# One uneven product for a Householder step, and the work laid around it

## The chip, the core and the metric

The kernel runs on one core of one Trainium2 chip. The core has five engines that run side by side and wait for each other by semaphores: TensorE (PE in the profile; its weight loads are shown apart, as PEld), VectorE (DVE), ScalarE (ACT), GpSimd (POOL) and SyncE (SP), which here issues the DMAs. The metric is the time of one execution on the device, in microseconds (us), as the median of several runs. All data are fp32, and an fp32 matmul is carried out as two passes, so the profile shows every product twice.

## The reference, cut to what matters

A stack of four graph layers works on `x` of 128 x 64 x 256. The stretch that is changed lies in layers 0 and 1:

```python
# layer 0: h = relu(layernorm(x))
agg = jnp.einsum('nm,bmd->bnd', A_hat, h)                 # "mix": 64 x 64 matrix over the nodes
h = relu(batchnorm(agg.reshape(-1, 256) @ W1.T + b1))     # 8192 rows, 256 -> 512
out = batchnorm(h @ W2.T + b2)                            # 512 -> 256
# layer 1: needs the eigenvectors of a 64 x 64 symmetric matrix
_, U = jnp.linalg.eigh(L_norm)
```

`L_norm` depends on the adjacency matrix alone, and layer 0 does not need `U`. Layer 1 needs both the result of layer 0 and `U`.

## The kernel before

**Two streams at once.** `eigenvectors` (line 1593) makes `U` while layer 0 is computed. The eigenvector work is a long chain of small operations on 64 x 64 matrices. First `tridiagonal` brings the matrix to tridiagonal form in 62 Householder steps (`householder`, line 1041, c = 63 down to 2). Then `vectors` (line 1426) finds the eigenvalues and eigenvectors, forms `U`, and `verdict` checks the result. At the end a value is loaded from the verdict, and all engines take a branch on it (line 1618), behind which layer 1 begins. Layer 0 is work with full-size products: for each of 16 blocks of 512 rows, `hidden_block` normalises (4 ScalarE operations), mixes (2 groups of 4 products with `BDH`), multiplies by `W1` (8 products of 512 columns), and takes the results out with 4 VectorE statistics and 4 ScalarE copies. When all 16 are done, and the batch statistics with them, `features0` does 8 products with `W2` for each block. In the profile these products are `ps<-BDH,z` and `ps<-z,w`.

**A Householder step.** The matrix `A` lies on 64 partitions. All 64 partitions of the row tiles hold the same row, so each partition can do the scalars of the step by itself. `x` is the current row of `A`. ScalarE squares and sums it and takes the square root `s0`. VectorE forms `r` = 1/s0, `t` = r·h + s0, `NB` = q·t (q is half the sign), corrects two elements of `x` with `OA` and `NB`, and takes a reciprocal, `KAP`. ScalarE makes `uk` = KAP·x. PE has meanwhile made two products with `A` over c rows: `z`, the row that is next, and `y` = xA, with the column of `A` that equals the row x as weights. VectorE combines them to `uA` = NB·z + y, sums uA·uk to `c2`, and makes `v` = c2·x - uA. Then come two things. PE makes the rank-two update as two products with one row each (K = 1), uk by v and v by uk, summed in PSUM, and VectorE adds that to `A`. And VectorE makes the next row by itself, in two updates of `z` with `uk` and `v`. Each step also stores its row x to `V` by a DMA on SP's queue (line 1064).

**What sets the order.** The order on PE, VectorE and ScalarE is written out ahead, by a planner (`Plan`, line 843). `chain` places the operations of the chain one after the other, each with an assumed busy time of its engine and an assumed time until its result is ready. Before each it fills the engine with pieces of layer 0 (`beside`), as far as they end no more than a slack after the chain's operation could start. The slacks are 0.6 us on T (PE), 0.3 on S (ScalarE) and 0.3 on V (VectorE). `emit` sorts all by the planned start and issues them, and each engine keeps that order (`Ordered`). These times only choose an order. What isn't placed by the end of the 62 steps is issued behind `vectors` (`rest`), where the order is not fixed by hand.

Of the kernel before, what the change touches and what calls it, by code (L numbers as in the profile page):

```python
# [8 lines left out]
F32 = mybir.dt.float32  # L9
# [775 lines left out]
GRID = 64  # L785

# [56 lines left out]
class Plan:  # L843
# [55 lines left out]

    def rest(self):  # L900

        while any(self.queue.values()):
            for e in self.queue:
                self.fill(e, 1e9)
# [8 lines left out]
class Fast:  # L913
# [31 lines left out]
    def sum(self, out, a, s, b, op0, op1=ALU.mult, name="junk"):  # L945

        w = a.shape[-1]
        j = self.t(f"{name}{a.shape[0]}", a.shape[0], 64)
        self.o.stt(j[:, 0:w], a, s, b, op0, op1, acc=out)
# [3 lines left out]
    def constants(self):  # L953
# [6 lines left out]
        self.P = t("P", 64, 1)  # L960
        iota(self.P[:], [[0, 1]], 0, 1)
# [21 lines left out]
        o.ts(self.low[:], self.J[:64, :], self.P[:], ALU.is_lt)  # L983
# [3 lines left out]
        o.copy(pi[:], self.P[:])  # L987
# [15 lines left out]
    def tridiagonal(self, S, made, plan):  # L1003
# [3 lines left out]
        A = self.A = t("A", 64, 64)  # L1007
# [3 lines left out]
        for x in (KAP, NB, V):  # L1011
            nc.vector.memset(x[:], 0.0)
        s0, r, tt, q, c2 = (t("h_" + x, 64, 1) for x in "s0 r t q c2".split())
        ja = t("ja", 64, 64)
        bc = lambda c, n=64: c.to_broadcast([n, 64])
        now = {}
        go = plan.chain

        def keep(name, a, b):
            now[name] = self.mm((a, b))  # L1020

        d = go("T", lambda: keep("p", S, self.JR[:]), [made], 0.3, 0.5)
        d = go("V", lambda: o.copy(m[:], now["p"][:]), [d], 0.15, 0.28)
        d = go("T", lambda: keep("p", self.JR[:], m[:]), [d], 0.3, 0.5)
        rest = go("V", lambda: o.copy(A[:], now["p"][:]), [d], 0.15, 0.28)
        d = go("T", lambda: keep("p", bc(ident[:64, 63:64]), A[:]), [rest], 0.3, 0.5)

        def first():
            x = now["x"] = self.rows.tile([64, 65], F32, name="f_x", bufs=8)
            o.copy(x[:, 0:63], now["p"][:, 0:63])  # L1030

        def square(w):
            x = now["x"]
            self.act(ja[:, 0:w], x[:, 0:w], AF.Square, accum_out=x[:, w:w + 1])

        row = go("V", first, [d], 0.15, 0.28)
        h = go("S", lambda: square(63), [row], 0.34, 0.42)
        for c in range(63, 1, -1):
            row, h, rest = self.householder(c, now, go, row, h, rest, (s0, r, tt, q, c2), square)

    def householder(self, c, now, go, row, h, rest, scalars, square):

        o, nc, t = self.o, self.nc, self.t
        ident = self.k.ident
        A, NB, OA, KAP, V = self.A, t("NB", 64, 64), t("OA", 64, 64, 2), t("KAP", 64, 64), t("V", 64, 64)
        s0, r, tt, q, c2 = scalars
        bc = lambda a, n=64: a.to_broadcast([n, 64])
        x = lambda a, b: now["x"][:, a:b]
        nb = NB[:, c - 1:c]
        e, w = 0.001 * c, c - 1  # L1050

        def zy():
            now["zp"] = self.ps.tile([64, 64], F32, name="fps")
            nc.tensor.matmul(now["zp"][:, 0:c], bc(ident[0:c, c - 1:c], c), A[0:c, 0:c], start=True, stop=True)
            now["yp"] = self.ps.tile([64, 64], F32, name="fps")
            nc.tensor.matmul(now["yp"][:, 0:c], bc(A[0:c, c:c + 1], c), A[0:c, 0:c], start=True, stop=True)

        def row_z():
            now["z"] = self.rows.tile([64, 64], F32, name="f_z")
            self.act(now["z"][:, 0:c], now["zp"][:, 0:c], AF.Copy)  # L1060

        def row_uk():

            nc.sync.dma_start(V[c:c + 1, 0:c], now["x"][0:1, 0:c])
            now["uk"] = self.rows.tile([64, 64], F32, name="f_uk")
            self.act(now["uk"][:, 0:c], x(0, c), AF.Copy, scale=KAP[:, c:c + 1])

        def row_uA():
            now["uA"] = self.rows.tile([64, 64], F32, name="f_uA")
            o.stt(now["uA"][:, 0:c], now["z"][:, 0:c], nb, now["yp"][:, 0:c], ALU.mult, ALU.add)  # L1070

        def row_v():
            now["v"] = self.rows.tile([64, 64], F32, name="f_v")
            o.stt(now["v"][:, 0:c], x(0, c), c2[:], now["uA"][:, 0:c], ALU.mult, ALU.subtract)

        def outer():
            uk, v = now["uk"], now["v"]
            p = now["p"] = self.ps.tile([64, 64], F32, name="fps")
            nc.tensor.matmul(p[0:c, 0:c], uk[0:1, 0:c], v[0:1, 0:c], start=True, stop=False)
            nc.tensor.matmul(p[0:c, 0:c], v[0:1, 0:c], uk[0:1, 0:c], start=False, stop=True)  # L1080

        def row_x():
            now["x"] = self.rows.tile([64, 65], F32, name="f_x", bufs=8)
            o.stt(x(0, w), now["uk"][:, 0:w], now["v"][:, w:c], now["z"][:, 0:w], ALU.mult, ALU.add)


        z = go("T", zy, [rest], 0.34, 0.42)
        sq = go("S", lambda: self.act(s0[:], x(c, c + 1), AF.Sqrt), [h], 0.13, 0.23)
        oa = go("S", lambda: self.act(OA[:, c, 1:2], x(c - 1, c), AF.Copy), [row], 0.12, 0.22)
        zs = go("S", row_z, [z], 0.15, 0.26 + e)  # L1090
        sg = go("V", lambda: o.ts(q[:], x(c - 1, c), **halve(0)), [row])
        d = go("V", lambda: o.recip(r[:], s0[:]), [sq])
        d = go("V", lambda: o.stt(tt[:], r[:], x(c, c + 1), s0[:], ALU.mult, ALU.add), [d, h])
        b = go("V", lambda: o.mul(nb, q[:], tt[:]), [d, sg])
        d = go("V", lambda: o.stt(x(c - 1, c + 1), OA[:, c, :], nb, x(c - 1, c + 1), ALU.mult, ALU.add), [b, oa])
        d = go("V", lambda: o.recip(KAP[:, c:c + 1], x(c, c + 1)), [d])
        uk = go("S", row_uk, [d], 0.16, 0.32 + e)
        d = go("V", row_uA, [zs, b, z], 0.12 + e, 0.25 + e)
        d = go("V", lambda: self.sum(c2[:], now["uA"][:, 0:c], 0.5, now["uk"][:, 0:c], ALU.mult), [uk, d],
               0.2 + e, 0.28 + e)  # L1100
        v = go("V", row_v, [d], 0.15 + e, 0.26 + e)
        p = go("T", outer, [v], 0.25, 0.45)
        if c > 2:
            row = go("V", row_x, [v], 0.15 + e, 0.22 + e)
            row = go("V", lambda: o.stt(x(0, w), now["v"][:, 0:w], now["uk"][:, w:c], x(0, w), ALU.mult, ALU.add),
                     [row], 0.15 + e, 0.25 + e)
            h = go("S", lambda: square(w), [row], 0.28 + e, 0.36 + e)
        rest = go("V", lambda: o.add(A[0:c, 0:c], A[0:c, 0:c], now["p"][0:c, 0:c]), [p], 0.12 + e, 0.22 + e)
        return row, h, rest

    def reflectors(self):
# [8 lines left out]
        self.sum(kc[:], self.KAPs[:], 1.0, ident, ALU.mult)  # L1120
# [22 lines left out]
    def scale(self):  # L1143

        o, nc, t = self.o, self.nc, self.t
        NB, A = t("NB", 64, 64), self.A
        self.KAPs = t("KAP", 64, 64)
        DM, NE = t("DM", 64, 64), t("NE", 64, 64)
        o.mul(DM[:], A[:], self.k.ident[:64, :64])
        pe = self.mm((self.k.ident[:64, 1:2].to_broadcast([64, 64]), A[:]))  # L1150
# [293 lines left out]
P = 128  # L1444
# [21 lines left out]
class Kernel:  # L1466
# [126 lines left out]
    def eigenvectors(self):  # L1593
# [3 lines left out]
        with ExitStack() as ex:  # L1597
            fast = Fast(self.tc, ex, self)
            fast.constants()
            plan = Plan(dict(T=0.6, S=0.3, V=0.3), 5)  # L1600
# [206 lines left out]
    def hidden_block(self, i, r, m, plan, needs, used):  # L1807
# [9 lines left out]
        def mix(dc):  # L1817
# [969 lines left out]
```

## Time and profile before

| what | us |
|---|---|
| median of 3 runs (lowest, highest) | 2329.3 (2326.33, 2331.57) |
| span of the profiled execution | 2325.1 |
| first row x copied, first Householder step begins | 11.5 |
| hidden features of layer 0 done (last product) | about 208 |
| last update of A by a step | 272.2 |
| verdict (f_k_badi) | 364.66 |
| first work behind the branch | 370.1 |
| PE busy / VectorE busy / ScalarE busy, of the span | 98% / 70% / 49% |

The profile shows one execution. In the tables of stretches, an engine's busy time counts every moment in which at least one of its instructions is under way. In the timeline each row is a start, a duration, an engine, a line, an operation, the tile that is written and the tiles that are read, and how many like it follow; in brackets stands how long the engine had been idle before, and what released it. Nearly all instructions have line 799, that of the helper which records the order, so tiles tell them apart: `fps` are the products of the chain, `f_x` the row, `f_h_r`, `f_h_t`, `f_NB`, `f_KAP` the scalars, `f_junk` the sum that gives c2, and `ps` the banks of layer 0.

### The profile page before, as it was taken

How to read it: one execution, taken by the hardware profiler on the slowest of the kernel's cores; microseconds unless marked ns; L12 is line 12 of the kernel's file. 1: busy time of each engine (PE TensorE's matmuls, PEld its weight loads, DVE VectorE, ACT ScalarE, POOL GpSimd, SP SyncE). 2: the span in 40 equal slices, each digit the busy share in tenths (PEclk: the TensorE clock that was granted, in tenths of full speed). 3: DMA queues.
4: the chain of work that ended last, by engine and by line, in shares of the span. 5: the costliest groups of instructions: out<-in, count | busy, mean ns of one | idle time of the engine just before them, and what ended most of it. 6: DMA issues, size and time to landing. Idle time of an engine off the chain costs nothing.

```text
span 2325.1 us, 32725 instructions
## 1 busy us (share of the span) xinstructions
PE 2283.6 (98%) x12169; PEld 1633.1 (70%) x12169; DVE 1629.3 (70%) x4054; ACT 1139.5 (49%) x2483; POOL 3.0 (0%) x26
## 2 busy tenths in 40 slices
PE   7999998999999999999999999999999999999999
PEld 4554445676777788888999998888885544554544
DVE  8887676888447777666767676559756686766667
ACT  5765865754436654433444444336435544444321
POOL 0000000000000000000000000000000000000000
PEclk9999999999999999999999999999999999999999
DMA  5000211230000000001000002000010000000001
GB/s 171 1 1 26 65 56 30 71 83 19 1 37 0 1 19 1 1 1 37 1 1 1 1 1 73 1 1 17 1 46 28 1 5 15 15 19 14 14 24 46
DMA packets 61065, 54.81 MB, mean 24 GB/s; under 512 B 15203, under 2 KB 58724, under 8 KB 60900
## 3 DMA queue, kind: packets, MB, share of 16 engines
q1 hardware_dynamic: 60900, 52.66, 7.4%
q8 instruction: 97, 1.59, 0.3%
q14 instruction: 68, 0.56, 0.1%
HBM read 35.86 MB, written 16.78 MB: 23 GB/s over the span
## 4 chain that ended last, share of the span: by engine, by line
PE 79%; DVE 3%; issue 1%; ACT 1%; DMA 0%; SPq 0%; ACTq 0%; DVEq 0%
PE ps L799 69%; PE acc L799 5%; PE pt L799 4%; PE pe L799 1%; PE y L799 1%; DVE aw L799 1%; DVE X L799 1%; DVE sm_m L799 0%; DVE XV L799 0%; ACT ls_g L799 0%; ACT h L799 0%; DVE ls_g L799 0%; ACT big L799 0%; DVE ls_t L799 0%; DVE sm_e L799 0%
## 5 line engine op out<-in xcount | busy, mean ns | idle before, releaser
L799 ACT ACTIVATE ls_g<-ls_g,ls_b 128x512 f32<-128x512 f32 (+4 forms) x472 | 243.1, 565 | 151.4 <-DVE ls_g L799 149.6
L799 ACT ACTIVATE ls_g<-ps,ls_b 128x256 f32<-128x256 f32 (+3 forms) x268 | 115.5, 470 | 330.9 <-PE ps L799 327.7
L799 PE MATMUL ps<-z,w 128*128 128x512 f32 x512 | 254.9, 621 | 0.9 <-ACT z L799 0.9
L799 PE MATMUL ps<-big,X 128*128 128x176 f32 (+3 forms) x848 | 212.7, 366 | 0.1
L799 DVE TENSOR_TENSOR ls_g<-ls_z,ps 128x512 f32<-128x512 f32 (+5 forms) x256 | 146.8, 579 | 91.9 <-PE ps L799 90.4
L799 DVE TENSOR_TENSOR aw<-at,ed_OST 128x1024 f32<-128x1024 f32 x128 | 149.9, 1219 | 83.0 <-PE ps L799 82.8
L799 PE MATMUL ps<-ls_tx,X 128*128 128x160 f32 (+2 forms) x960 | 206.8, 326 | 0.6 <-ACT ls_g L799 0.6
L799 PE MATMUL ps<-X,X 128*128 128x160 f32 (+1 forms) x896 | 199.1, 306 | 0.0
L799 PE MATMUL ps<-X,ls_w 128*128 128x256 f32 x640 | 190.5, 379 | 0.0
L799 PEld LDWEIGHTS ps<-ls_tx,X 128*128 128x128 f32 x960 | 161.8, 190 | 15.1 <-DVE X L799 4.8
L799 PEld LDWEIGHTS ps<-big,X 128*128 128x128 f32 x848 | 145.9, 190 | 29.7 <-issue 19.4
L799 DVE TENSOR_TENSOR X<-ls_g 128x1024 f32<-128x1024 f32 (+2 forms) x108 | 117.4, 1087 | 49.9 <-ACT ls_g L799 49.8
L799 ACT ACTIVATE r<-ps 128x512 f32<-128x512 f32 x256 | 131.6, 614 | 41.5 <-PE ps L799 41.4
L799 PEld LDWEIGHTS ps<-X,X 128*128 128x128 f32 x896 | 148.4, 190 | 0.0
L799 PE MATMUL ps<-X,ls_s 128*128 128x256 f32 x480 | 142.3, 379 | 0.0
L799 PEld LDWEIGHTS ps<-z,w 128*128 128x128 f32 x512 | 87.2, 190 | 69.0 <-issue 60.2
L799 PE MATMUL ps<-ls_tx,ls_s 128*128 128x256 f32 x464 | 134.8, 379 | 0.0
L799 PE MATMUL ps<-ed_S,Q 64*128 64x512 f32 x512 | 132.9, 618 | 1.4 <-DVE hT L799 0.7
L799 PE MATMUL ps<-ls_tx,ls_w 128*128 128x256 f32 x464 | 133.2, 380 | 0.0
L799 PEld LDWEIGHTS ps<-X,ls_w 128*128 128x128 f32 x640 | 121.4, 190 | 16.8 <-DVE X L799 0.3
L799 PE MATMUL ps<-big,ls_w 128*128 128x256 f32 x464 | 131.9, 379 | 0.7 <-ACT ls_z L799 0.7
L799 PE MATMUL ps<-aw,ed_ODT 128*64 128x512 f32 x512 | 117.3, 595 | 0.1
(545 smaller groups left out, 4019.0 us busy)
## 6 DMA issues: line engine op xcount, KB each, us to landing
X<-in_x_dram SPq DMA_DIRECT2D x32, 512.0 KB
xs<-X SPq DMA_DIRECT2D x16, 512.0 KB
X<-xs SPq DMA_DIRECT2D x16, 512.0 KB
out_dram<-X SPq DMA_DIRECT2D x31, 256.0 KB
X<-in_L_gnn_Wih_t_dram SPq DMA_DIRECT2D x4, 512.0 KB
ls_w<-in_L_gnn_Wih_t_dram SPq DMA_DIRECT2D x4, 512.0 KB
ls_w<-in_L_gnn_Whh_t_dram SPq DMA_DIRECT2D x4, 512.0 KB
w<-in_L_gnn_W_t_dram SPq DMA_DIRECT2D x2, 512.0 KB
```

Of the source, the lines that this page charges most:

```text
L799: i = method(*a, **kw)
```

## The change

The step is rewritten, and with it the planner's use and the size of the pieces.

- The update is one product over 65 rows. `left` has KAP·x in row 0 and -uA in row 64, `right` has v in row 0 and KAP·x in row 64; all other rows of `left` are zero. Three of the four rows are written by ScalarE copies of one partition each (`side`). `v` is written by VectorE on all 64 partitions, straight into `right`. The sum `dd` uses KAP as its scalar and x in place of uk.
- `A` has 65 rows, the last of them zero, and z and y are products over 65 rows, into one PSUM tile. As y no longer stops at row c, its column is a copy `xc` in which the rows from c on are zero. One small VectorE operation a step makes the next `xc` from the product and `A`, with a mask `MK`.
- `t` goes: `NB` = r·(q·h) + q·s0, where ScalarE makes q·s0. The next row starts with uk and uA (`row_x1`), and v enters in the second update. The copy to `OA` moves from ScalarE to POOL.
- `uk`, `z`, `uA` have one buffer in place of two, the rows x six in place of eight.
- Pieces of layer 0 are halved: a mix is two pieces of two products; products of 512 columns become two of 256.
- For each step, `weigh` lays the step out 27 times with different slacks, scores each layout by the busy time placed on each engine less 2.7 times its end, and keeps the best. This happens when the program is built.

```diff
+    def weigh(self, make, slacks, worth, cost):
+        free, queue = dict(self.free), {e: list(v) for e, v in self.queue.items()}
+        n, k = len(self.steps), len(self.opened)
+        best = None
+        for slack in [*slacks, None]:
+            self.slack = slack or best[1]
+            made = make()
+            if slack is None:
+                return made
+            gain = sum(x.busy * worth.get(x.engine, 0.0) for x in self.steps[n:])
+            gain -= cost * max(x.at + x.ready for x in made)
+            if best is None or gain > best[0]:
+                best = gain, slack
...
+        self.slacks = [dict(T=a, S=b, V=v, P=0.0) for a in (0.2, 0.45, 0.8) for b in (0.1, 0.3, 0.6) for v in (0.1, 0.35, 0.65)]
...
         for c in range(63, 1, -1):
-            row, h, rest = self.householder(c, now, go, row, h, rest, (s0, r, tt, q, c2), square)
+            row, h, rest = plan.weigh(lambda: self.householder(c, now, go, row, h, rest),
+                                      self.slacks, dict(T=1.0, S=0.5, V=2.0), 2.7)
...
+        def products():
+            zy = now["zy"] = self.ps.tile([R, 2, 64], F32, name="fps")
+            for i, column in enumerate((self.k.ident[0:R, c - 1:c], xc[:])):
+                nc.tensor.matmul(zy[:, i, 0:c], column.to_broadcast([R, R]), A[:, 0:c], start=True, stop=True)
...
+        def side(out, a, scale):
+            self.act(out, a[0:1, 0:c], AF.Copy, scale=scale)
 
         def outer():
-            uk, v = now["uk"], now["v"]
-            p = now["p"] = self.ps.tile([64, 64], F32, name="fps")
-            nc.tensor.matmul(p[0:c, 0:c], uk[0:1, 0:c], v[0:1, 0:c], start=True, stop=False)
-            nc.tensor.matmul(p[0:c, 0:c], v[0:1, 0:c], uk[0:1, 0:c], start=False, stop=True)
+            p = now["p"] = self.ps.tile([P, 64], F32, name="fps")[:R]
+            nc.tensor.matmul(p[:, 0:c], left[:, 0:R], right[:, 0:c], start=True, stop=True)
...
+        zy = go("T", products, [rest], 0.5, 0.7)
+        sq = go("S", lambda: self.act(s0[:], x(c, c + 1), AF.Sqrt), [h], 0.13, 0.25)
+        oa = go("P", lambda: nc.gpsimd.tensor_copy(OA[:, c, 1:2], x(c - 1, c)), [row], 0.2, 0.4)
+        sg = go("V", lambda: o.ts(q[:], x(c - 1, c), **halve(0)), [row], 0.09, 0.25)
+        g = go("V", lambda: o.mul(qh[:], q[:], x(c, c + 1)), [sg, h], 0.09, 0.25)
+        d = go("V", lambda: o.recip(r[:], s0[:]), [sq], 0.09, 0.25)
+        qr = go("S", lambda: self.act(qs[:], s0[:], AF.Copy, scale=q[:]), [sq, sg], 0.13, 0.25)
+        zs = go("S", row_z, [zy], 0.14, 0.27 + e)
+        b = go("V", lambda: o.stt(nb, r[:], qh[:], qs[:], ALU.mult, ALU.add), [d, g, qr], 0.09, 0.25)
...
+        uA = go("V", row_uA, [b, zy, zs], 0.12 + e, 0.25 + e)
+        sides = [go("S", lambda: side(left[64:65, 0:c], now["uA"], -1.0), [uA], 0.14, 0.27 + e)]
+        k = go("V", lambda: o.recip(kap, x(c, c + 1)), [d], 0.09, 0.25)
+        uk = go("S", row_uk, [k], 0.16, 0.32 + e)
+        sides += [go("S", lambda out=out: side(out, now["x", c], KAP[0:1, c:c + 1]), [k], 0.14, 0.27 + e)
+                  for out in (left[0:1, 0:c], right[64:65, 0:c])]
+        d = go("V", lambda: self.sum(dd[:], now["uA"][:, 0:c], kap, x(0, c), ALU.mult), [uA, k], 0.2 + e, 0.28 + e)
+        v = go("V", lambda: o.stt(right[0:64, 0:c], x(0, c), dd[:], now["uA"][:, 0:c], ALU.mult, ALU.subtract),
+               [d], 0.12 + e, 0.26 + e)
         if c > 2:
+            row = go("V", row_x1, [uk], 0.12 + e, 0.26 + e)
+        p = go("T", outer, [v] + sides, 0.25, 0.45)
+        if c > 2:
+            row = go("V", lambda: o.stt(nx(0, w), right[0:64, 0:w], now["uk"][:, w:c], nx(0, w), ALU.mult, ALU.subtract),
+                     [row, v], 0.12 + e, 0.25 + e)
+            h = go("S", lambda: self.square(now["x", w], w), [row], 0.28 + e, 0.36 + e)
+            m = go("V", lambda: o.stt(xc[0:64], now["p"][0:64, w:c], A[0:64, w:c], self.MK[:, w:c], ALU.add, ALU.mult),
+                   [p], 0.09, 0.25)
         rest = go("V", lambda: o.add(A[0:c, 0:c], A[0:c, 0:c], now["p"][0:c, 0:c]), [p], 0.12 + e, 0.22 + e)
...
-            x = beside("T", lambda dc=dc: mix(dc), h, 0.98, 1.1, bank)
+            x = beside("T", lambda dc=dc: mix(dc, 0), h, 0.5, 0.6, bank)
+            x = beside("T", lambda dc=dc: mix(dc, 1), [x], 0.5, 0.66)
...
-            x = beside("T", lambda hc=hc: product(hc, 0), mixed, 0.86, 0.9, bank)
-            x = beside("T", lambda hc=hc: product(hc, 1), [x], 0.86, 1.0)
+            x = beside("T", lambda hc=hc: product(hc, 0, 0), mixed, 0.43, 0.43, bank)
+            for k, kc in ((0, 1), (1, 0), (1, 1)):
+                x = beside("T", lambda hc=hc, k=k, kc=kc: product(hc, k, kc), [x], 0.43, 0.6 if k and kc else 0.43)
```

## The prediction

> **What bounds the kernel now.** The execution that was profiled spans 2325.1 us; the runs have a median of 2329.3 us (2326.3 to 2331.6), 4.2 us more. Sums are made against the span, and the same difference is laid on the median. Two medians within 0.2% (4.7 us) can't be told apart here. Everything that the change touches ends before 372 us, where layer 1 begins, so I read that stretch alone: first the busy time by stretches (columns: stretch, its length, then busy time and instructions of PE, weight loads, VectorE, ScalarE, POOL, then the granted clock and the DMA share).
>
> ```profile
> 30.00:80.00 50.00, 48.95 (x234) 26.64 (x232) 40.11 (x192) 35.54 (x115) 0.00 (x0) 1.00 0.08 15
> ...
> 220.00:272.00 52.00, 50.90 (x201) 20.98 (x201) 29.80 (x188) 44.24 (x149) 0.00 (x0) 1.00 0.27 80
> ```
>
> PE is busy throughout (the stretches left out: 48.20 and 50.00 of 50 up to 180 us, 66.55 of 68 from 272 to 340). Up to 209 us layer 0 makes its hidden features beside the Householder steps (45 steps from 11.5 us: 4.39 us each), up to 272 us its second product beside the last 17 steps (3.7 us each), then the rest of it beside the eigenvector work. A busy PE may be a PE that waits for its own pipeline, so next the timeline of one step (start, duration, engine; each matmul is two passes, "x2"):
>
> ```profile
> 100.35 3.70 PE L799 MATMUL ps<-z,w 128*128 128x512 f32 x8
> 103.98 0.27 PE L799 MATMUL fps<-f_v,f_uk 1*44 1x44 f32 x2
> 104.09 0.25 PE L799 MATMUL fps<-f_uk,f_v 1*44 1x44 f32 x2
> 104.26 1.13 PE L799 MATMUL ps<-z,w 128*128 128x512 f32 x2
> 105.32 0.31 PE L799 MATMUL fps<-f_A,ident 43*64 43x43 f32 x2
> 105.46 0.29 PE L799 MATMUL fps<-f_A 43*64 43x43 f32 x2
> 105.67 2.84 PE L799 MATMUL ps<-z,w 128*128 128x512 f32 x6
> ```
>
> ```profile
> 103.03 0.19 PEld L799 LDWEIGHTS ps<-z,w 128*128 128x128 f32 x1 [0.24 <-issue]
> 103.98 0.15 PEld L799 LDWEIGHTS fps<-f_v,f_uk 1*44 1x44 f32 x2 [0.76 <-issue]
> ...
> 111.10 0.86 PEld L799 LDWEIGHTS ps<-BDH,z 128*128 128x128 f32 x7 [0.24 <-issue]
> ```
>
> A 512-column pass comes every 0.43 us. Eight of them are 3.44 us, but 3.63 us pass until the small product starts (100.35 to 103.98): 0.19 lost. Two are 0.86, but 1.06 pass (104.26 to 105.32): 0.20 lost. The small products take 0.28 (103.98 to 104.26) and 0.35 (105.32 to 105.67). So **each step costs PE 1.02 us** outside layer 0. The loads show where the lost 0.2 goes: ahead of a small product the load stands idle 0.76 us, 0.52 more than between two full-size products, though nothing is named that it waits for; between full-size products of different length (BDH) it is 0.24 as ever.
>
> Last the chain of the step itself, where little stands between: VectorE's timeline in one step.
>
> ```profile
> 198.41 0.15 DVE L799 RECIPROCAL f_h_r<-f_h_s 64x1 f32<-64x1 f32 x1 [0.43 <-ACT f_h_s L799]
> 198.60 0.21 DVE L799 SCALAR_TENSOR_TENSOR f_h_t<-f_h_r,f_x,f_h_s 64x1 f32<-64x1 f32 x1
> 198.85 0.15 DVE L799 TENSOR_TENSOR f_NB<-f_h_q,f_h_t 64x1 f32<-64x1 f32 x1
> 199.10 0.21 DVE L799 SCALAR_TENSOR_TENSOR f_x<-f_OA,f_NB,f_x 64x2 f32<-64x2 f32 x1
> 199.35 0.15 DVE L799 RECIPROCAL f_KAP<-f_x 64x1 f32<-64x1 f32 x1
> 199.43 0.23 DVE L799 SCALAR_TENSOR_TENSOR f_uA<-f_z,f_NB,fps 64x20 f32<-64x20 f32 x1
> 199.88 0.17 DVE L799 SCALAR_TENSOR_TENSOR f_junk<-f_uA,f_uk 64x20 f32<-64x20 f32 x1 [0.23 <-ACT f_uk L799]
> 199.99 0.07 DVE L799 DVE_READ_ACCUMULATOR f_junk<-f_uA,f_uk 64x1 f32 x1
> 200.10 0.23 DVE L799 SCALAR_TENSOR_TENSOR f_v<-f_x,f_h_c,f_uA 64x20 f32<-64x20 f32 x1
> ```
>
> ScalarE's part of it starts at 197.83 (square), 198.18 (sqrt) and 199.54 (uk). From start to start: square to sqrt 0.35, to the reciprocal 0.23, to h_t 0.19, to NB 0.25, to KAP 0.50, to uk 0.19, to the sum 0.34, to v 0.22; then the two row updates and the next square at 0.27 each (192.94, 193.21, 193.48 in the step before): 3.08 us. The real step is 1.3 us longer up to 209 us. So the chain is stretched by what is laid between, and PE, which never idles, is the limit.
>
> The end of the stretch has two parties: the last layer-0 pass runs out near 364.5 us, and the verdict on the eigenvectors (f_k_badi, 364.66) lets the branch go only at 370.1; PE stands 5.5 us for it. A gain must come to both.
>
> **The change, part by part.**
>
> *One product for the update, all products over 65 rows.* Removed: two of four passes in the update. The others change shape, 65x65 instead of at most 64x64; no row has that shape. The Trainium skill (TensorEngine Tiling (Array Packing), Key Properties) says that a change of tiling mode drains TensorE, while a change of tile within a mode doesn't, and its modes have 32, 64 or 128 rows. The rows agree: 0.2 lost at each entry to a small shape, none into BDH, which is full size. By that rule 65 rows can only be full size, so the drain goes. By the rows alone the bounds are: below, a pass of 0.055 us (loads of f_A, two in 0.11) and no drain, 6 x 0.055 plus 0.05 at each of two exits = 0.43 us a step; above, the BDH row's 0.11 a pass and the drain kept, 0.66 + 0.40 = 1.06, no gain. I take 0.43: 0.59 saved a step.
>
> *Chain.* h_t goes (NB straight from the reciprocal, with ScalarE's q·s0 beside it), and the first row update no longer waits for v: after KAP uk 0.19, first update 0.34, second 0.27, as against 0.19 + 0.34 + 0.22 + 0.27 + 0.27. The loop falls by 0.25 + 0.49 = 0.74 to 2.34 us. The other loop (uA, sum, v, update, A, z/y, z copied, uA) gets longer by the row copies and the masked column. From like rows: four ScalarE operations to the product 0.9, product 0.35, mask and add 0.32, z/y 0.45, copy 0.24, uA 0.22: 2.5 us, so it sets the pace. Neither reaches today's 3.08, so the chain is worth nothing by itself; it lets the PE gain through.
>
> *VectorE*: 13 operations a step instead of 12, about 0.1 us more. It is busy 40.11, 40.83 and 40.87 of 50 us in the three stretches from 30 to 180 us, 81% or 3.57 of 4.39 us a step. With PE's 0.59 gone a step would be 3.80, and VectorE 3.67 of it: 96%. I let it run at 93%, a step of 3.94: **0.45 kept, x 45 = 20 us.** *ScalarE* issues four more operations and one less. Those with a scale from memory take 0.19 to the next issue (uk), others 0.11: q·s0 0.19, rows 0.11 + 0.19 + 0.19, less OA's 0.11: +0.57 a step. From 220 to 272 us it is busy 44.24 of 52 us, 3.16 of a step's 3.7; with 0.57 more it is full at 3.73. **The last 17 steps gain 0.** Behind 272 us nothing changes.
>
> *POOL copies OA.* No POOL copy is in the trace; its fills and iotas of 64x1 take 0.09 to 0.13 us. It is wanted 0.35 + 0.23 + 0.19 + 0.25 = 1.02 us after its input (with the square's start, for the x that follows NB). Against it speaks the skill (GPSIMD Engine Reference, Specifications): POOL shares its SBUF interfaces with VectorE and contends with operations of two SBUF inputs, which most of the step's are. By the row it costs 0; by the rule it may stand behind VectorE operations, at most a 0.69 us statistics pass: 0.13 + 0.69 is still under 1.02. I take 0; if a copy took 1.3 us the cost would be 0.28 x 62 = 17 us.
>
> *Finer pieces.* Passes of 256 columns instead of 512. Later in the trace four such passes load within 0.84 us, 0.21 each, half of 0.43: no cost on PE. Their gain, less waiting of a small product behind a pass, is in the step assumed. *Weighed layouts* only choose the written order, at no run time. Bound: a better order than today's can't fill a PE that is full; a worse one is the third case below.
>
> *Six row buffers for eight.* The first row store is issued at 34.88 us, behind the loads of x; the first buffer is wanted again in the 6th step, at about 11.5 + 6 x 3.9 = 35. Between 0 and 3 us, once; I take 1. New constants ahead of the first step (a comparison and the first masked column): 0.3.
>
> Sum: 20 - 1.3 = 19 us, for the layer-0 stream and (20 us earlier steps) for verdict and branch alike. Span 2306, **median 2310 us**.
>
> **The rivals.**
>
> *All of it comes through (2294 us).* VectorE and ScalarE overlap more than busy time says, the last steps shed work to the stretch behind: 62 x 0.59 = 37 less 1.3. For: busy time counts an operation's latency. Against: 96% and 100%.
>
> *VectorE and ScalarE take PE's place (2326 us).* The order laid out favours a short chain and leaves PE idle, or 65 rows still drain: only the two passes go, 2 x 0.055 x 62 = 7 us, and waits take half. For: both are near full.
>
> *Slower (2341 us): the row copies set the pace.* The update waits for the last of uk and three row copies. If a layer-0 piece of 0.58 to 0.80 us on ScalarE stands between KAP and the last copy in each step, and another ahead of the z copy, the second loop is 2.5 + 1.5, plus two waits for a pass in flight on PE (0.2 each): 4.4 us. It decides from 4.21 on, today's mean of (272.4 - 11.5)/62 steps; 0.2 x 62 = 12 us slower. Against: VectorE's instruction is as often what is late today.
>
> **How the numbers follow.** Forecast 0.49 (own range 2301 to 2318), all of it 0.13, taken place 0.20, slower 0.18. The third case straddles the bound: 0.12 faster, 0.06 same, 0.02 slower. Faster 0.74, same 0.06, slower 0.20. The range 2295 to 2333 leaves out half of the second case and about three quarters of the slower one, which reaches from 2330 to beyond 2350.
>
> **What would show it.** Ahead of fps products the load idle 0.76 becomes about 0.24, and a step's two pauses in the z,w passes fall from 1.02 to about 0.45 us. Up to the end of the hidden features a step takes about 3.9 us; the last update of A stands near 252 us, f_k_badi near 345. VectorE's share rises above 90%, ScalarE's near 100% in the last steps. Wrong if PE shows idle time ahead of the fps products that is named by the ScalarE row copies, or if the drain stays.

## The result, and the profile after

The changed kernel takes **5599.3 us** (5596.8 to 5600.5), the kernel before 2330.4 us on the same chip (2326.3 to 2331.7): a ratio of 2.405, with a 95% interval of 2.401 to 2.409. The forecast of 2310 us is wrong by more than any of its cases allowed for. The profiled execution spans 5595.0 us.

The page of the kernel after says at once that this isn't a matter of single microseconds. Its second part, the busy tenths in 40 slices of the span (140 us each), and one group of its fifth part:

```profile
PE   7881110000000000000000000099999999999999
...
DVE  7767778888888888888888899876676666766766
...
PEclk9995555555555555555555555599999999999999
...
L122 PE MATMUL eps<-e_left,e_ones 64*64 64x1 f32 x2 | 0.4, 252 | 2179.3 <-DVE e_left L45 2179.3
```

From slice 4 to slice 26 PE does next to nothing, at half the clock, and it stands for 2179 us ahead of one product alone. VectorE meanwhile works on tiles that begin with `e_`. No such tile is in the profile before. They belong to the other side of the branch on the verdict, `holds.Else`, where the class `Eig` works out the eigenvectors anew by a slow method. The timeline of the kernel after shows the way into it and out of it:

```profile
386.11 0.15 DVE L800 CAST f_k_badi<-fps 64x1 int32<-64x1 f32 x1 [0.64 <-PE fps L800]
...
400.52 0.11 DVE L148 MEMSET e_ones<- 64x64 f32 x1 [14.26 <-ACT big L800]
...
3637.72 0.68 PE L800 MATMUL ps<-U,I 64*128 64x64 f32 x2 [0.31 <-DVE UT L65]
...
3639.51 3.69 PE L800 MATMUL ps<-ones,ident 128*128 128x128 f32 x16 [0.69 <-DVE BDUT L800]
```

The verdict is cast to an integer at 386.1 us, the fallback starts at 400.5, and layer 1 begins at 3639.5 instead of 370.1. **So the new step makes numbers that the verdict turns down, and all but some 30 of the 3269 us are the fallback.** The rest is the shared stretch, which got slower, too. The stretches of the kernel after, in the columns of the prediction's first fence:

```profile
30.00:80.00 50.00, 40.59 (x234) 32.59 (x234) 38.49 (x183) 41.31 (x134) 1.77 (x10) 0.97 0.09 16
...
220.00:272.00 52.00, 41.82 (x254) 32.29 (x254) 34.10 (x198) 41.38 (x147) 2.30 (x13) 1.00 0.14 41
```

PE was busy for 48.95 of the 50 us before and is for 40.59 now. VectorE is no fuller than before (38.49 against 40.11). The timeline of one step in the kernel after:

```profile
104.20 0.19 PEld L800 LDWEIGHTS fps<-f_R,f_L 65*65 65x65 f32 x2 [0.53 <-ACT big L800]
104.23 0.28 PE L800 MATMUL fps<-f_R,f_L 65*65 65x45 f32 x2 [0.37 <-DVE f_R L800]
104.32 0.53 PEld L800 LDWEIGHTS ps<-BDH,z 128*128 128x128 f32 x4
...
106.11 0.19 PEld L800 LDWEIGHTS fps<-f_A,ident 65*65 65x65 f32 x2 [1.26 <-issue]
106.14 0.28 PE L800 MATMUL fps<-f_A,ident 65*65 65x44 f32 x2 [1.10 <-DVE f_h_q L800]
...
106.34 2.66 PEld L800 LDWEIGHTS ps<-z,w 128*128 128x128 f32 x8
```

From the first load of the update to the next load of layer 0 it is 0.12 us (104.20 to 104.32), and for z and y 0.23 us (106.11 to 106.34). The products became as cheap as forecast, 0.35 us in a step. But ahead of them PE now waits, 0.37 and 1.10 us here, and these waits have names.

### The profile page after: what moved, and what is told of

The parts are those of the page before. It is cut to its first block, busy times and chain, and to the rows that moved or that the text cites. A ratio compares the mean times of both kernels' runs of the same rounds, so it can differ in the third digit from the quotient of the medians.

```text
span 5595.0 us, 57174 instructions
## 1 busy us (share of the span) xinstructions
PE 2356.8 (42%) x12862; PEld 1771.5 (32%) x12862; DVE 4328.8 (77%) x23282; ACT 1359.2 (24%) x3477; POOL 14.6 (0%) x95
## 5 line engine op out<-in xcount | busy, mean ns | idle before, releaser
L457 ACT ACTIVATE e_q_r_y<-e_q_r_hh 64x1 f32<-64x1 f32 x540 | 109.7, 203 | 1357.3 <-DVE e_q_r_hh L51 1234.7
L800 PE MATMUL ps<-z,w 128*128 128x256 f32 x1024 | 257.5, 396 | 1.2 <-DVE f_h_q L800 0.6
L68 DVE RECIPROCAL e_q_r_r<-e_q_r_y 64x1 f32<-64x1 f32 x540 | 83.6, 155 | 153.6 <-ACT e_q_r_y L457 150.9
L800 PEld LDWEIGHTS ps<-z,w 128*128 128x128 f32 x1024 | 187.6, 193 | 26.3 <-ACT z L800 2.9
L800 PEld LDWEIGHTS ps<-ls_tx,X 128*128 128x128 f32 x960 | 161.8, 190 | 15.4 <-DVE X L800 5.0
```

The costliest lines, as they stand in the source:

```text
L68: self.v.reciprocal(o, a)
L457: nc.scalar.activation(y[:], hh[:], AF.Sqrt)
L800: i = method(*a, **kw)
```

## The experiments

Two questions had to be settled: why the verdict says no, and what the step costs without the fallback. I took the first for a matter of accuracy, and two of the first three runs seemed to bear that out. It was wrong. The expectations call the explanations that they set against each other theories, each with a letter. e3, e8, e9, e13 and e14 were executed once; what they have to tell apart is some 3200 us.

### Which condition, and is it accuracy?

**A lower threshold for the sign (e1), the column from the row (e2), a higher threshold in the kernel before (e3).** The verdict joins eight conditions. One of them wants the sign of each eigenvector certain, by the size of a sum over the middle coupling.

```diff
-        o.ts(cand[:], aa[:], 3e-4 * root, ALU.is_lt)
+        o.ts(cand[:], aa[:], 2e-4 * root, ALU.is_lt)
...
-        o.ts(g1[:], aa[:], 3e-4 * root, ALU.is_ge)
+        o.ts(g1[:], aa[:], 2e-4 * root, ALU.is_ge)
```

> The kernel after, with one number changed: the size from which the sign of an eigenvector is taken as certain (the sum over the middle coupling) is 2e-4 instead of 3e-4 times the root of 2. Nothing else moves. Theory D (the uneven update drifts: its rounding makes row and column of A differ, one eigenvector's sum falls under 3e-4, that one condition sends all engines into the fallback): the fallback goes, and what is left is the slower shared stretch, in which the verdict came 386.1 - 364.7 = 21 us later than before: 2330 + 21 = 2351 us (2343 to 2360). Theory B (the new step computes something wrong, by a stale row or a copy to partition 64): several conditions fail, this number is one of many, and the time stays 5599 us.

Measured: 5598.5 us, ratio 2.404 (2.400 to 2.408). The fallback stayed. Theory D, as put here, missed.

```diff
-            m = go("V", lambda: o.stt(xc[0:64], now["p"][0:64, w:c], A[0:64, w:c], self.MK[:, w:c], ALU.add, ALU.mult),
-                   [p], 0.09, 0.25)
+            m = go("V", lambda: self.sum(xc[0:64], nx(0, w), 1.0, self.k.ident[0:64, 0:w], ALU.mult), [row], 0.2 + e, 0.28 + e)
```

> The kernel after, with one VectorE instruction of each step exchanged: the column for the next y product is taken from the next row itself (its diagonal, summed against the identity) and not from A plus the product, so that row and column can't differ. Threshold as in the kernel after. Theory D: the drift goes with the difference of row and column, no fallback, 2345 us (2335 to 2360): the same stretch, the exchanged instruction some 0.1 us longer but no longer behind the product. Theory B, or a drift that comes from the uneven product alone: the fallback stays, 5599 us.

Measured: 2358.9 us (2357.6 to 2360.4), ratio 1.0133 (1.0116 to 1.0150). The fallback is gone. That looked like the proof of theory D and was none, as e14 shows.

```diff
-        o.ts(cand[:], aa[:], 3e-4 * root, ALU.is_lt)
+        o.ts(cand[:], aa[:], 4e-4 * root, ALU.is_lt)
...
-        o.ts(g1[:], aa[:], 3e-4 * root, ALU.is_ge)
+        o.ts(g1[:], aa[:], 4e-4 * root, ALU.is_ge)
```

> The kernel before, with the same number raised to 4e-4. Worked through in double precision the reference's matrix has one eigenvector with a sum of 5.2e-4, above 3e-4 times the root of 2 (4.24e-4) and below 4e-4 times it (5.66e-4), whose second sum has the other sign. Theory D: the condition fails here too and the fallback runs behind an unchanged stretch: 2330 + (5599 - 2330 - 21) = 5578 us (5560 to 5595). If that eigenvector isn't what decides, 2330 us.

Measured: 5567.0 us, against 2327.7 us for the kernel before on this chip. This gives the price of the fallback: **3239 us**. The traces put it some 4 us lower, as the verdict stood at 369.5 us in this execution and at 364.7 in that of the kernel before: from the verdict to layer 1's first product it is 3610.3 - 369.5 = 3240.8 us here and 5.5 us there, a difference of 3235 us.

**The sign condition left out (e4).**

```diff
-        o.copy(ok[:], self.signed[:])
+        o.copy(ok[:], self.one[:, 0:1])
```

> The kernel after, with the sign condition left out of the verdict (it starts from one; every other condition stays). After the run with 2e-4, where the fallback stayed, theory D holds only if the drift moves the sum further than to 2.83e-4: then this condition alone decides and the fallback goes, 2351 us (2343 to 2360). Theory B, or a drift so large that other conditions fail as well: 5599 us.

Measured: 5604.5 us. At least one more condition fails, so a sum that is a little too small can't be the whole story.

**Which ones (e8, e9).** Every condition, and four bounds on the difference between A and its transpose, get a branch of their own ahead of the verdict's; the side taken on failure fills a tile that carries the condition's name.

```diff
+            v = nc.values_load(fast.fi[0:1, 7:8], min_val=0, max_val=64)
+            with self.tc.If(v < 1, preferred_fallthrough_block=False, label="is_orthogonal") as h:
+                pass
+            with h.Else():
+                nc.vector.memset(fast.t("failed_orthogonal", 64, 1)[:], 0.0)
```

> The kernel after, with twelve small branches ahead of the one on the verdict: one for each of the eight conditions, and one each for a largest difference between A and its transpose (rows keep the values that they had when their step began) above 1e-6, 1e-5, 1e-4 and 1e-3. A branch that fails fills a tile of its own name, which the trace then shows. The run with the sign condition left out kept the fallback, so at least one other fails. Theory D (drift of the uneven update): the differences pass 1e-6 at least, in the kernel on the chip far more than the 1.4e-7 that single precision worked through by hand gives, and residual, gap or sign fail. Theory B (reflectors or their copies wrong): the reflector or the orthogonality condition fails. Time 5599 us and 12 branches of 1 to 5 us: 5610 to 5660 us.

> The same twelve branches in the kernel with the column taken from the row. Theory D: no condition fails, the differences stay a class or more smaller than in the kernel after, 2358.9 us and 12 branches: 2370 to 2420 us. Should the differences be as large as in the kernel after, it is not the drift of A but the mismatch of column and row in one step that counts.

Measured: 5611.0 us and 2366.1 us, the second just under its range. The trace of e8 holds two of the twelve tiles (each line is the answer for one tile):

```profile
L800 DVE MEMSET f_failed_signed<- x1: 59/59/59, 390.8 to 390.8; 64x1 f32 x1
...
L800 DVE MEMSET f_failed_orthogonal<- x1: 59/59/59, 410.1 to 410.1; 64x1 f32 x1
```

In e9 none of the twelve was filled. In the changed kernel the sign and the orthogonality fail (an entry of UᵀU - I above 2e-5), while the other six conditions hold (residual, gap, couplings and reflectors among them), and A agrees with its transpose within 1e-6. The difference doesn't measure every kind of error, but the drift that I had in mind would have shown there: not one of its four bounds was passed, in either kernel. Theory D had lost its mechanism. Theory B had foretold the orthogonality condition, and was still open.

**The same matrix with other last digits (e12, e13, e14).** The eigenvectors of a matrix and of its multiple are the same, and the kernel scales the tridiagonal matrix to a fixed interval anyway. Only the rounding of all that follows changes. The edit is one instruction, in the kernel after, the kernel before (0.99999895), and e2's kernel (1.0000003):

```diff
-        rest = go("V", lambda: o.copy(A[0:64], now["p"][:]), [d], 0.15, 0.28)
+        rest = go("V", lambda: o.ts(A[0:64], now["p"][:], 1.000002, ALU.mult), [d], 0.15, 0.28)
```

> The kernel after, in which the copy that first fills A multiplies by 1.000002. The eigenvectors of a scaled matrix are the same; only the last digits of all that follows differ. Theory D (the new step's arithmetic drifts): the fallback stays, 5599 us. Theory R (the last digits decide: in one of the 64 vectors a cancellation comes out as an exact zero, and the vector is lost): this draw comes out well, no fallback, and what is left is the slower stretch, 5599 - (5567 - 2328) = 2360 us (2352 to 2366).

> The kernel before, in which the copy that first fills A multiplies by 0.99999895; nothing else is changed. Theory D: no fallback, 2329 us. Theory R: the old step falls as well with the wrong last digits, and this draw is one of those: 5567 us (5560 to 5575).

> The kernel with the column taken from the row (2358.9 us, no fallback), in which the copy that first fills A multiplies by 1.0000003. Theory D (that the column from the row mended the drift): no fallback, 2359 us. Theory R (it only drew other digits): this draw falls, 5600 us (5590 to 5610).

Measured: e12 **2364.7 us** (2361.8 to 2368.0), ratio 1.0156 (1.0138 to 1.0173); e13 **5569.5 us**; e14 **5596.3 us**. All three as theory R has it. Theory B falls as well: e12 has the same copies, products and tiles as the kernel after, and passes. The changed step passes its verdict with other last digits, and the old step fails with other last digits, with the fallback at the same price (5569.5 - 2328.9 = 3241 us; in the changed kernel 5599.3 - 2364.7 = 3235 us). The change didn't break the eigenvectors and e2 didn't mend them: **each drew new digits, and which side of the branch the kernel takes hangs on them.** What loses a vector was argued and not measured: worked through in single precision by the kernel's formulas, the recurrence that gives one vector's entries ends in terms with a few significant bits left, and in some draws one of them is exactly zero, at which the vector is anchored in the wrong place. The expectations named the side for each of the three factors beforehand, which speaks for this working; it also means that the factors are no random sample. How often a vector is lost, for either step, these runs can't say.

### What the step costs without the fallback

e12 is the changed kernel with the branch going the usual way: 2364.7 us, 35.7 more than before. The stretch from 11 to 345 us in the kernel before and in e12, in the same columns:

```profile
11.00:345.00 334.00, 322.68 (x1416) 163.43 (x1417) 251.34 (x1254) 228.73 (x730) 0.00 (x0) 0.99 0.16 47
11.00:345.00 334.00, 285.03 (x1603) 227.03 (x1604) 240.11 (x1216) 256.79 (x852) 11.05 (x62) 0.96 0.14 40
```

The 30 us from 40 on in e12:

```profile
40.00:70.00 30.00, 26.59 (x134) 22.06 (x134) 23.92 (x115) 23.28 (x75) 1.01 (x6) 0.84 0.00 1
```

The waits of PE up to 300 us (what waited, for what; us in total, how often, the longest):

```profile
PE fps L800 <- DVE f_x L800: 20.2, 19, 2.5
PE fps L800 <- DVE f_h_q L800: 19.2, 27, 1.1
PE fps L800 <- ACT f_R L800: 6.0, 9, 1.7
```

What released the engines that had to do with `f_R`, the side of the update that holds v (us, times):

```profile
  ACT f_R L800: 46.1, 53
```

And PE's timeline, with the end of the layer-0 stream in the kernel before (first) and in e12 (last):

```profile
360.72 3.70 PE L799 MATMUL ps<-z,w 128*128 128x512 f32 x8
...
46.91 3.25 PE L800 MATMUL ps<-z,w 128*128 128x256 f32 x14
...
65.47 0.32 PE L800 MATMUL fps<-f_R,f_L 65*65 65x53 f32 x2 [1.83 <-DVE f_x L800]
...
66.87 6.19 PE L800 MATMUL ps<-z,w 128*128 128x256 f32 x14
...
399.64 2.97 PE L800 MATMUL ps<-z,w 128*128 128x256 f32 x13
```

PE stands idle for 334 - 285.03 = 49.0 us; in the kernel before it was 334 - 322.68 = 11.3 us. The 53 waits for `f_R` are 44 of the weight load (40.2 us, part of them behind work still under way on PE) and 9 of the product itself (6.0 us): in most of the 62 updates ScalarE's last row copy is what the load waits for last. The waits that the list puts down to `f_x` can hide the same copy: at 65.47 us load and product start together, the load named as waiting for `f_R`, whose copy ends at 65.42, and the product for `f_x`, which ends at 65.44. `f_h_q` is the operation that VectorE issues right behind the update of A, which z and y read. And idle PE costs twice: the same 14 passes take 3.25 us at 46.9 and 6.19 us at 66.9, behind a stretch of short work and waits, and the granted clock of 40 to 70 us is 0.84. The layer-0 stream's last pass on PE ends at 402.6 us (before: 364.4), 13 us behind the verdict at 389.5.

The next runs ask what of the new step does that. All but e7 start from e2's kernel (2358.9 us), whose stretch is nearly e12's. After each of these changes the planner lays all steps out anew, so each difference holds the edit together with the order that came of it.

**Fixed slacks instead of the weighed layouts (e5).**

```diff
-            row, h, rest = plan.weigh(lambda: self.householder(c, now, go, row, h, rest),
-                                      self.slacks, dict(T=1.0, S=0.5, V=2.0), 2.7)
+            row, h, rest = self.householder(c, now, go, row, h, rest)
```

> The kernel with the column taken from the row (2358.9 us), laid out with the fixed slacks of the kernel before (0.6, 0.3, 0.3) and not weighed. Theory L (the weighed layout puts statistics passes of layer 0 between nearly all operations of the chain, some 4 us of them in the step from 102 to 107 us): the step gets shorter by about 0.5 us, 2358.9 - 30 = 2329 us (2310 to 2335). Theory C (ScalarE's row copies set the pace; PE stands 48 us for the last of them): the copies are as many, 2352 to 2362 us.

Measured: 2376.1 us, ratio 1.0209 (1.0190 to 1.0227): 17 us slower still, which neither theory had, and theory L falls. The loop did get shorter, with A's last update at 268.1 us instead of 304.2, but the stream got longer, to 412.1 us, with PE idle for 57.3 us up to 345 us instead of 45.4 and a granted clock of 0.90 instead of 0.97. That the statistics between the chain's operations were what kept the stream going is likely, and not shown by itself.

**Two row copies on POOL (e6).**

```diff
-        sides += [go("S", lambda out=out: side(out, now["x", c], KAP[0:1, c:c + 1]), [k], 0.14, 0.27 + e)
+        sides += [go("P", lambda out=out: nc.gpsimd.tensor_copy(out, now["uk"][0:1, 0:c]), [uk], 0.2, 0.3 + e)
                   for out in (left[0:1, 0:c], right[64:65, 0:c])]
```

> The kernel with the column taken from the row, still weighed; the two copies of the scaled row (to partitions 0 and 64) are made by POOL from the scaled row, not by ScalarE. Theory C: ScalarE has 0.64 us less to do in a step and the update waits for two POOL copies of some 0.2 us instead: about 0.4 us less in each of 62 steps, 2335 us (2325 to 2345). Theory L: the copies are not what is waited for, 2350 to 2362 us.

Measured: 2338.4 us, ratio 1.0044 (1.0029 to 1.0058): 20.5 us less than e2, as theory C has it. In the timeline a copy takes POOL 0.21 us; it took ScalarE 0.31 to 0.33:

```profile
106.94 0.21 POOL L1132 COPY f_L<-f_uk 1x44 f32<-1x44 f32 x1 [3.74 <-ACT f_uk L800]
...
107.20 0.21 POOL L1132 COPY f_R<-f_uk 1x44 f32<-1x44 f32 x1
...
107.47 0.19 PEld L800 LDWEIGHTS fps<-f_R,f_L 65*65 65x65 f32 x2 [0.39 <-POOL f_R L1132]
```

So the two copies on ScalarE, with the order that they bring, are the larger part of the loss, 20 of some 30 us. What was won is not the wait for the last copy, though: that stayed (48.2 us in 60 waits for ScalarE's `f_R` in e2, 40.7 us in 53 for POOL's in e6). What fell is ScalarE's work in the step: from 11 to 345 us it is busy for 239.5 us instead of 263.5, and A's last update comes at 272.9 us instead of 304.2.

**The old chain in the old fixed order, but no drains and no row copies (e7).** The kernel before, with 65-row products for z and y, and the update as two products over 64 equal rows:

```diff
-            nc.tensor.matmul(p[0:c, 0:c], uk[0:1, 0:c], v[0:1, 0:c], start=True, stop=False)
-            nc.tensor.matmul(p[0:c, 0:c], v[0:1, 0:c], uk[0:1, 0:c], start=False, stop=True)
+            nc.tensor.matmul(p[:, 0:c], uk[:, 0:R], v[:, 0:c], start=True, stop=False)
+            nc.tensor.matmul(p[:, 0:c], v[:, 0:R], uk[:, 0:c], start=False, stop=True)
...
-        rest = go("V", lambda: o.add(A[0:c, 0:c], A[0:c, 0:c], now["p"][0:c, 0:c]), [p], 0.12 + e, 0.22 + e)
+        rest = go("V", lambda: o.stt(A[0:c, 0:c], now["p"][0:c, 0:c], 1.0 / 64, A[0:c, 0:c], ALU.mult, ALU.add), [p],
+                  0.12 + e, 0.25 + e)
```

> The kernel before with its own chain, its own fixed order, 512-column pieces and the OA copy on ScalarE, but all small products over 65 rows: z and y as in the kernel after, the update as its two products over all 64 equal copies of the rows (the sum is 64 times too large and is scaled by 1/64 where A is updated), and the column for y from the next row by one VectorE sum. No row copies. By the prediction's reckoning PE saves its drains: 1.02 us a step becomes 8 passes of 0.055 and two exits of 0.05, 0.54, and VectorE gets 0.25 us more: about 0.2 to 0.3 kept of each of 62 steps, 2315 us (2308 to 2325). If PE was never the limit of the step: 2328 to 2345 us, by the added sum on VectorE. If adding 64 equal rows rounds too coarsely: some 5570 us.

Measured: 2384.4 us, ratio 1.0241 (1.0222 to 1.0261). None of the expectations had that. The updates of A:

```profile
L800 DVE SCALAR_TENSOR_TENSOR f_A<-fps,f_A x62: 146/180/216, 17.1 to 256.7; 63x63 f32<-63x63 f32 x1, 62x62 f32<-62x62 f32 x1, 61x61 f32<-61x61 f32 x1, 60x60 f32<-60x60 f32 x1
```

A stretch of its steps:

```profile
100.00:209.00 109.00, 88.23 (x412) 50.02 (x411) 82.67 (x473) 56.70 (x227) 0.00 (x0) 0.77 0.01 1
```

And PE's timeline behind the verdict:

```profile
359.91 68.93 PE L800 MATMUL ps<-z,w 128*128 128x512 f32 x160
```

The steps did become faster: 3.93 us each ((256.7 - 17.1) / 61), the last update 15.5 us earlier than before, and the verdict 4.7 us earlier, at 360.0. But in these shorter steps less of layer 0 was carried, PE stood idle for 53 us up to 345 us and ran at a granted clock of 0.77 in the stretch shown, and 160 passes of layer 0 were left for the time behind the verdict. The stream ended at 428.8 us. The clock is as large a part of this as the idle time: up to the stream's end PE is idle for 40 us more than in the kernel before, and at a granted clock of 0.89 over that time its 365 busy us hold, as an estimate, 0.11 x 365 = 40 us of slower passes. A faster chain brings nothing if the order lays less work beside it.

**All copies on POOL, and layouts weighed for PE (e10, e11).**

```diff
-        sides = [go("S", lambda: side(left[64:65, 0:c], now["uA"], -1.0), [uA], 0.14, 0.27 + e)]
+        sides = [go("P", lambda: nc.gpsimd.tensor_scalar(left[64:65, 0:c], now["uA"][0:1, 0:c], -1.0, None, ALU.mult), [uA], 0.2, 0.3 + e)]
...
-                                      self.slacks, dict(T=1.0, S=0.5, V=2.0), 2.7)
+                                      self.slacks, dict(T=2.0, S=1.0, V=1.0), 2.7)
```

> As the run with two copies on POOL (2338.4 us), with the third copy (minus uA) on POOL too, and the layouts weighed for TensorE's filling (worths 2, 1, 1 for TensorE, ScalarE, VectorE in place of 1, 0.5, 2). In that run the layer-0 stream on PE ended at 376 us, 11 us behind the verdict (365), with PE idle for 32 us up to 345. Theory P (PE's idle time in the steps is the loss, and filling it pays one to one): the written layout leaves some 10 us less of it, 2329 us (2320 to 2336). Theory C alone (ScalarE's copies): 0.24 us less on ScalarE for each step, at most 5 us: 2333 to 2338.

> As the run with two copies on POOL, only the worths changed (3, 0.5, 1 for TensorE, ScalarE, VectorE). Theory P: the written layout leaves 8 us less of PE idle and the loop ends later while the stream ends earlier: 2331 us (2322 to 2338), with verdict and stream closer together; the verdict may become the later one, near 380 us, and then nothing is gained: 2338 to 2350.

Measured: e10 2327.2 us, ratio 0.9995 (0.9986 to 1.0004); e11 2331.5 us, ratio 1.0011 (1.0002 to 1.0020). Both as theory P has it. e10 changes two things at once; e11 against e6 (2338.4 us) shows the worths alone, 7.0 us. In both the verdict became the later party: e10's stream ends at 349.2 us and its verdict stands at 364.4, e11's at 350.2 and 370.8. So e10 had 15 us of stream in hand.

**The two parties balanced (e15).**

```diff
-                                      self.slacks, dict(T=2.0, S=1.0, V=1.0), 2.7)
+                                      self.slacks, dict(T=2, S=1, V=1), 3.2)
```

> As the run with all three copies on POOL (2327.2 us), where the loop ended at 274.8 us, the verdict stood at 364.4 and the layer-0 stream had already ended at 349: only the price of a late step in the weighing is higher (3.2 for 2.7), so the loop should end some 10 us earlier and the stream some 2 us later. Theory P (the later of verdict and stream sets the end, and TensorE's idle time in the loop is what each gain is paid with): 2318 us (2313 to 2324). If the loop's end doesn't follow the written order: 2325 to 2329.

Measured: **2322.8 us**, ratio **0.9978** (0.9970 to 0.9987): 6 us less than the kernel before, a small difference that twelve runs set clear of the noise. The loop ends 10 us earlier, as expected, but the stream ends 10 us later than in e10 and not 2. Its stretch from 11 to 345 us:

```profile
11.00:345.00 334.00, 306.52 (x1788) 254.71 (x1789) 264.81 (x1424) 234.70 (x735) 56.33 (x248) 0.99 0.17 48
```

The verdict, from the answer for its tile:

```profile
L800 DVE CAST f_k_badi<-fps x1: 151/151/151, 354.2 to 354.2; 64x1 int32<-64x1 f32 x1
```

And the end of the stream in PE's timeline:

```profile
354.12 5.45 PE L800 MATMUL ps<-z,w 128*128 128x256 f32 x24
```

The verdict is 10.5 us earlier than before. The stream's last pass ends at 359.6 us, 4.8 us earlier than before, and as the later of the two it sets the end. This kernel takes the usual side of the branch by the luck of its digits, as all of them do.

The runs side by side; PE idle is 334 us less the busy time from 11 to 345 us:

| kernel | last update of A | verdict | stream's last pass ends | layer 1 begins | PE idle | clock, 11 to 345 us | median |
|---|---|---|---|---|---|---|---|
| before | 272.2 | 364.7 | 364.4 | 370.2 | 11.3 | 0.99 | 2329 |
| after, other digits (e12) | 299.6 | 389.5 | 402.6 | 406.7 | 49.0 | 0.96 | 2364.7 |
| column from the row (e2) | 304.2 | 394.1 | 396.8 | 401.3 | 45.4 | 0.97 | 2358.9 |
| e2, fixed slacks (e5) | 268.1 | 365.7 | 412.1 | 414.2 | 57.3 | 0.90 | 2376.1 |
| e2, two copies on POOL (e6) | 272.9 | 365.4 | 375.9 | 380.7 | 32.4 | 0.97 | 2338.4 |
| before, no drains (e7) | 256.7 | 360.0 | 428.8 | 431.0 | 53.0 | 0.86 | 2384.4 |
| three copies on POOL (e10) | 274.8 | 364.4 | 349.2 | 369.5 | 20.2 | 1.00 | 2327.2 |
| the same, balanced (e15) | 264.4 | 354.2 | 359.6 | 363.7 | 27.5 | 0.99 | 2322.8 |

Layer 1's first product comes 2.1 to 5.5 us behind the later of the verdict and the stream's end. From that product on each of these eight executions takes 1954.6 to 1957.2 us, so its start holds the whole difference between them.

## Why the prediction was wrong, point by point

**The step that failed is a sentence: "Behind 272 us nothing changes."** It held the verdict's branch for a wait of 5.5 us with one way out. The branch has another side, and its price stood nowhere in the profile before, because it hadn't been taken. The change rewrites the arithmetic on which the branch decides: the form of `NB`, the update's two halves, the column for y, the sum for `dd`. That alone was enough. The missing rival is "the new digits fail the verdict"; its place was on record (line 1618 and the verdict's conditions), its price could not be read from the trace, and it decides from a single lost vector on. Of 3269 us lost it explains 3235 to 3241, by e12, e3 and e13.

Without it, too, the forecast was on the wrong side: 2364.7 us (e12) instead of 2310. Its steps:

- *PE is the limit, a step costs it 1.02 us and will cost 0.43.* The cost after was right, and with 65 rows the drain did go: 0.35 us for the products themselves. In e10, 20 passes of 256 columns and one step's products stand between the loads at 123.09 and 127.87: 4.78 - 20 x 0.215 = 0.48 us with the exits.
- *"0.59 saved", of which 0.45 kept.* That is where the sum failed. PE's saved time became idle time: 49.0 us instead of 11.3. From 11 us to the end of the stream PE is busy for 340.8 us in the kernel before and for 339.6 us in e12, although some (1.02 - 0.48) x 62 = 33 us of drains and small passes are gone. A granted clock of 0.96 instead of 0.99 accounts for some 10 us of it (0.03 x 334). Another 16 us or so, estimated from the traces, are a matter of counting: an idle gap starts only where the pass ahead of it has ended, on average 0.25 us after a next pass could have followed, and e12 has 82 such gaps up to the end of the stream where the kernel before has 15 (20 us against 4). Some 7 us stay open.
- *Chain: "Neither reaches today's 3.08".* The second loop was put at 2.5 us, with the row copies back to back. The real step is (299.6 - 15.4) / 61 = 4.66 us. ScalarE's pieces and VectorE's statistics lie between the links, and three copies of 0.2 to 0.3 us hang on the way to a product for which PE, in its fixed order, waits.
- *VectorE, "I let it run at 93%".* It runs at 77% (38.49 of 50 us). It was never the next limit, nor was ScalarE, "full at 3.73" in the last 17 steps: in the kernel after these run from 225.8 to 296.4 us, 4.15 us each, and it is busy for 58.48 of the 70.60 us, 83%.
- *POOL copies OA at no cost.* Right. The copy takes 0.178 to 0.180 us in all 62 steps of e12, so nothing of the contention that was weighed against it shows in its duration, and nobody waits for it. POOL would have been the better place for two of the row copies as well, as e6 shows.
- *Finer pieces cost nothing.* Right for the passes: in e6, 86 of them lie in 18.83 us, 0.219 us each.
- *"Weighed layouts only choose the written order, at no run time".* True, and beside the point. The order decides how much of layer 0 is carried by a step: taking the weighing away costs 17 us (e5), other worths gave 7.0 us (e6 to e11), and another price for a late end 4.4 us (e10 to e15).
- *Rivals.* "The row copies set the pace" was the nearest mechanism, as e6 shows, and the sign of being wrong that was named came: idle time of PE ahead of the `fps` products that is named by the row copies. I gave it 0.18 and 2341 us, since I had the wait at one piece of ScalarE in a step, and left out the colder clock and the stream behind the verdict. "VectorE and ScalarE take PE's place" had PE idle for the wrong reason: neither was full.

## What to carry to other kernels

Before pricing a change to arithmetic, look for a branch that reads its result: a value loaded from a tile on all engines at once is one. Then put in a rival for its other side, even where that has never been seen, and try the same kernel with the input scaled by several factors a few parts in a million off one, which tells a change of method from a change of digits. And where two streams share in-order engines, time saved on the full engine is worth what the written order lays in its place: read both ends (here the verdict and the stream's last pass) and PE's idle time, not the chain's length.

## What the runs showed of the hardware

*The clock falls without a long pause.* The Trainium skill (TensorE: Matmul & The Clock Gate, HAM oscillation) warns of idle gaps of PE above about 3.4 us, and its Part 1 gives two states, half rate and full rate. The two states are here: 14 passes in 3.25 us, then in 6.19. But no gap that long stands ahead of the fall. The longest wait of PE on the step's products that e12's trace lists is 2.5 us, and the gap just ahead of the slow passes is 1.83, between short pieces of work. From 62.58 to 65.99 us PE is busy for 1.39 of 3.41 us, at a granted clock of 1.00; from 65.99 to 72.81 us it is busy for 6.38 of 6.82, and the granted clock is 0.50. Five more falls of e12 between 38 and 282 us stand behind 3.41 us with 1.51 to 1.76 us of work. So in this kernel a stretch that is about half filled is enough, though not every one: behind 270.80 to 274.21 us, as thinly filled, the clock stays at 1.00. e10 runs at 1.00 from 25 to 345 us, with PE busy for 95% of it, and e7, with PE idle for a fifth of the time, at 0.77 from 100 to 209 us.

*A row copy is cheaper on POOL than on ScalarE only in one form.* A row of 44 elements copied as it stands took POOL 0.21 us (e6), while ScalarE's copy with a scale read from memory took 0.33 (e12). The copy with a constant factor, minus uA, took ScalarE 0.228 us in the median of e12's 62 steps, and POOL 0.295 in e10's.
